# One register read per expert tile, moved into the step before it, in a graph-attention and mixture-of-experts kernel

## The chip, the cores and the metric

The kernel runs on one core of a Trainium2 chip. A core has five engines with an instruction queue each: TensorE (PE; its weight loads are listed as PEld), VectorE (DVE), ScalarE (ACT), GpSimd (POOL) and SyncE (SP). Each has a sequencer of its own that reads the instructions in their order; what the sequencer does itself, such as loading a register, is listed with a q (PEldq). The metric is the device time of one launch in microseconds, the median of several runs. A profiled execution gives the trace.

## The reference

A graph-attention layer with two heads over 6250 nodes and 100,000 edges, then a feed-forward layer in which each node goes to one of eight experts. Cut to what matters here:

```python
x = x + gat(layernorm(x), edges)               # segment sums over each node's edges
h = gelu(layernorm(x) @ W1 + b1)               # 6250 x 1024
probs = softmax(h @ Wg + bg)                   # over 8 experts
e = argmax(probs)
x = x + probs[e] * (h @ Wd[e] + bd[e])         # Wd: 8 x 1024 x 256, e differs from row to row
```

## The kernel before

The nodes are worked through in 49 blocks of 128. For each block GpSimd gathers the rows of its edges into `wg` in three parts of five, five and four tiles; VectorE and ScalarE weigh them (`weigh`); TensorE adds them up with a one-hot matrix (`add_up`, line 833) in PSUM. Small steps on the side find out which edges belong to the block: `prefix` (line 650, three matmuls of one column), `prefix_out` (653), `split` (662 on), `gather_late` (738), `choose` (745 to 756) and `spread` (761).

Four blocks make a phase. When a phase is summed, its rows go through the first feed-forward product (`g_hidden`, 916), the choice of expert (`g_logits` 954 to `g_place`) and are turned by TensorE (`g_rows`, 1039), copied by ScalarE (1040) and scattered to `by_expert`, a table in DRAM in which each expert has a list of its own. Full tiles of 128 rows of one expert are then taken out of it again, a phase later. `tabulate` makes, with VectorE, the table of the tiles that are ready: `where` (the tile's first row) and `who` (its expert). There are 55 such expert tiles: 1, then four a phase, and 14 in the last phase. For each, four steps run: `w_load` loads the rows (1126), `w_turn` turns them in two halves (1039, 1040), `w_expert` multiplies them by the expert's weights (1144 and 1146) and `w_out` makes the result `y` with VectorE (1160). In float32 a product shows as two passes in the profile, so the eight products of line 1146 are 16 matmuls.

Which expert it is, is known on the chip alone. So `w_expert` reads from `who` two numbers into registers of TensorE: the place of the expert's weights (line 1137) and of its bias (line 1140). The matmuls take their right-hand sides at these addresses, with a register instruction ahead of each (FUSED_REGOPS).

The order on every engine is written out by hand. `at(slot, place, fn, ...)` puts a step into a plan; the plan is sorted by slot and place, and the steps are called in that order, which is the order of every engine's queue. A block takes three slots, a phase twelve. `w_turn` has place 21, `w_expert` place 22 of the next slot, `add_up` place 32, `prefix` place 43. In the last phase no adding up is left, and turning and product alternate.

All of `w_turn`, `w_expert`, `g_rows`, `g_hidden` and `prefix` write to PSUM tiles named `pf`, of which there are three. A step that takes one over waits for its last reader.

## Time and profile before

| | us |
|---|---|
| median of 3 runs (lowest, highest) | 1330.88 (1330.65, 1338.22) |
| the profiled execution's own time | 1333.08 |
| its span, first to last instruction | 1331.3 |
| L1146 PE, products by expert weights, x880 | 204.6 busy |
| L833 PE, adding up, x1372 | 337.8 busy |
| L1144 PE, bias product, x55: TensorE idle before it | 8.0 in all: 5.5 "ACT wg L824", 1.4 "DVE idx L1158", 0.6 "DVE full_i L1068", 0.5 others |
| L761 PE: TensorE idle before it | 30.8, 17 times |
| mean granted TensorE clock | 0.934 |

A line of the timeline has the start, the duration, the engine, the line of the program, the operation, the tiles written and read, the number of instructions, and in brackets how long the engine stood idle before it and what ended that. Durations of the sequencer's own instructions are in the listings of single lines, as minimum, median and maximum in ns. The idle time named last in a list of waits is that of the semaphore that came last; it can be another's.

### The profile page before, as it was taken

How to read it: one execution, taken by the hardware profiler on the slowest of the kernel's cores; microseconds unless marked ns; L12 is line 12 of the kernel's file. 1: busy time of each engine (PE TensorE's matmuls, PEld its weight loads, DVE VectorE, ACT ScalarE, POOL GpSimd, SP SyncE). 2: the span in 40 equal slices, each digit the busy share in tenths (PEclk: the TensorE clock that was granted, in tenths of full speed). 3: DMA queues.
4: the chain of work that ended last, by engine and by line, in shares of the span. 5: the costliest groups of instructions: out<-in, count | busy, mean ns of one | idle time of the engine just before them, and what ended most of it. 6: DMA issues, size and time to landing. Idle time of an engine off the chain costs nothing. (4 is left out here: it accounts for less than half of the span.)

```text
span 1331.3 us, 22611 instructions
## 1 busy us (share of the span) xinstructions
PE 1133.9 (85%) x6551; PEld 873.9 (66%) x6551; DVE 971.6 (73%) x3521; ACT 679.9 (51%) x2011; POOL 840.3 (63%) x941
## 2 busy tenths in 40 slices
PE   4784677887978989989989899899898997998995
PEld 3563666665665775867757758677677586675784
DVE  6995889878797787877877977778779788651210
ACT  4782355546545546464565564555554646555221
POOL 1005777777777777777777776677766776626461
PEclk9796698898988999999999999899999998998998
DMA  4764866665555656665656566656566666646870
GB/s 147 227 193 122 234 186 187 205 191 171 174 171 183 216 178 200 195 205 174 207 170 204 177 205 189 192 175 189 183 190 198 181 196 195 191 128 231 293 236 16
DMA packets 115977, 249.77 MB, mean 188 GB/s; under 512 B 23372, under 2 KB 69656, under 8 KB 115702
## 3 DMA queue, kind: packets, MB, share of 16 engines
q0 software_dynamic: 44192, 131.04, 32.5%
q1 hardware_dynamic: 64342, 110.14, 26.5%
q10 hardware_dynamic: 7312, 7.05, 1.6%
q8 instruction: 56, 0.92, 0.3%
q14 instruction: 75, 0.61, 0.2%
HBM read 196.90 MB, written 57.97 MB: 191 GB/s over the span
## 5 line engine op out<-in xcount | busy, mean ns | idle before, releaser
L792 POOL DMA_INDIRECT wg<-table,dsti x686 | 675.1, 984 | 239.3 <-issue 169.7
L833 PE MATMUL p_a<-wg,hot 128*128 128x258 f32 x1372 | 337.8, 394 | 0.0
L833 PEld LDWEIGHTS p_a<-wg,hot 128*128 128x128 f32 x1372 | 263.7, 198 | 47.1 <-issue 9.2
L826 ACT ACTIVATE wg<-wg 128x128 f32<-128x128 f32 x686 | 216.6, 390 | 4.8
L916 PE MATMUL pf<-xT,w_sb 128*128 128x512 f32 (+1 forms) x416 | 199.4, 628 | 22.6 <-ACT xT L908 22.6
L1146 PE MATMUL pf<-wd_sb,half 128*128 x880 | 204.6, 386 | 0.0
L1146 PEld LDWEIGHTS pf<-wd_sb,half 128*128 128x128 f32 x880 | 162.7, 190 | 35.2 <-issue 10.1
L824 ACT COPY wg<-fix 128x10 f32<-128x10 f32 x147 | 25.0, 170 | 272.2 <-DVE wg L823 238.6
L916 PEld LDWEIGHTS pf<-xT,w_sb 128*128 128x128 f32 x416 | 81.2, 210 | 109.6 <-issue 80.1
L809 DVE TENSOR_TENSOR hot<-fix,loc 128x640 f32<-128x640 f32 x147 | 112.3, 764 | 25.1 <-ACT wg L824 24.6
L823 DVE TENSOR_TENSOR wg<-wg,fix 128x640 f32<-128x640 f32 x147 | 114.1, 776 | 5.1
L738 PE MATMUL pm<-rest,pick 128*128 128x33 f32 x588 | 82.2, 294 | 15.0 <-DVE place_i L666 15.0
L1040 ACT COPY half<-pf 128x512 f32<-128x512 f32 x110 | 60.8, 583 | 65.5 <-PE pf L1146 33.8
L918 ACT ACTIVATE hT<-pf,b_sb 128x512 f32<-128x512 f32 (+1 forms) x104 | 67.7, 659 | 47.1 <-PE pf L916 46.6
L1060 POOL DMA_INDIRECT by_expert<-row,place_i x47 | 49.4, 1052 | 65.3 <-ACT half L1040 18.3
L738 PEld LDWEIGHTS pm<-rest,pick 128*128 128x128 f32 x588 | 77.8, 211 | 15.7 <-issue 15.7
L456 PE MATMUL pf<-w_sb,xT 128*128 128x260 f32 x196 | 59.7, 432 | 18.6 <-ACT xT L450 18.6
L1040 ACT COPY row<-pf 128x512 f32<-128x512 f32 x94 | 52.3, 586 | 40.6 <-PE pf L1039 39.6
L1039 PE MATMUL pf<-ident,hT 128*128 128x128 f32 x392 | 59.0, 289 | 14.5 <-ACT row L1040 13.2
L704 ACT ACTIVATE wt<-tm,hot_e 128x128 f32<-128x128 f32 x196 | 66.4, 386 | 9.2 <-DMA tm<-terms 9.2
L619 POOL DMA_INDIRECT win<-keys,first x49 | 50.1, 1022 | 32.7 <-DMA keys<-keyb 14.2
L662 DVE TENSOR_SCALAR pick<-iota_s,late 128x768 f32<-128x768 f32 x49 | 30.8, 628 | 48.8 <-ACT late L653 48.8
(274 smaller groups left out, 1794.0 us busy)
## 6 DMA issues: line engine op xcount, KB each, us to landing
row<-by_expert SPq DMA_DIRECT2D x39, 641.0 KB
lbc<-lrow SPq DMA_DIRECT2D x49, 448.0 KB
wg<-table,dsti POOLq DMA_INDIRECT x686
wg<-by_expert SPq DMA_DIRECT2D x16, 641.0 KB
wd_sb<-in_L_ffn_Wd_dram SPq DMA_DIRECT2D x8, 1024.0 KB
tm<-terms SPq DMA_DIRECT2D x49, 128.0 KB
table<-tb ACTq DMA_DIRECT2D x12, 520.0 KB
xs<-in_x_dram SPq DMA_DIRECT2D x12, 512.0 KB
```

Source lines behind the costliest of these rows:

```text
L456: nc.tensor.matmul(pW[:, :TW], xT[:, k * P:(k + 1) * P], w_sb[:, k, :], start=(k == 0), stop=(k == KC - 1))
L704: nc.scalar.activation(kept[b]["wt"][:, g, h, :], tm[:, h, :], AF.Identity, scale=hot_e[:, g, 1, h:h + 1])
L738: nc.tensor.matmul(pk[:, c, :], k["pick"][:, c * P:(c + 1) * P], k["rest"], start=True, stop=True)
L792: nc.gpsimd.indirect_dma_start(out=wg[:, t - QS[q], :], out_offset=None, in_=table[:, :], in_offset=bass.IndirectOffsetOnAxis(ap=kept[b][" ...
L809: nc.vector.tensor_tensor(hot[:, :n], iota_ps.unsqueeze(1).to_broadcast([P, n, P]), kept[b]["loc"][:, QS[q]:QS[q + 1]].unsqueeze(2).to_bro ...
L823: nc.vector.tensor_mul(wg[:, :, :D], wg[:, :, :D], p_w[:, :, 0:1].to_broadcast([P, n, D]))
L826: nc.scalar.activation(wg[:, t, D2:SE], wg[:, t, D2:SE], AF.Identity, scale=wg[:, t, D + 1:D2])
L833: nc.tensor.matmul(sums[b], hot[:, t - QS[q], :], wg[:, t - QS[q], :SE], start=(t == 0), stop=(t == T - 1))
L916: nc.tensor.matmul(ph[:, :w], wt["w1"][:, k, j * P:(j + 1) * P], xT[:, k, :w], start=(k == 0), stop=(k == KC - 1))
L918: nc.scalar.activation(hT[:, j, :w], ph[:, :w], AF.Gelu, bias=wt["b1"][:, j:j + 1])
L1040: nc.scalar.copy(o, pT)
L1146: nc.tensor.matmul(py[:, :C], res[k]["half", i, j // 4][:, j % 4, :], wt["wd"][:, ds(wo[0] + j * C, C)], start=False, stop=(j == KH - 1))
```

## The change

`who` keeps one number per tile, the expert's number times C (256). It serves as the bias' place, and eight times it, worked out in the register instructions, as the weights' place. So TensorE reads one register per expert tile, in `w_ask`. This read is called at one of three places:

- A step at place 31.9 of the slot in which the tile is turned, one slot before its product, puts the tile on the list `asked`. The next `add_up` reads the register after its third product and empties the list.
- If no `add_up` came in between, `w_expert` reads it itself, ahead of its products.
- In the last phase the tiles but the first stand in the set `follows`: their register is read inside the product of the tile before, ahead of its sixth product of eight.

```diff
@@ add_up
             for t in range(QS[q], QS[q + 1]):
                 nc.tensor.matmul(sums[b], hot[:, t - QS[q], :], wg[:, t - QS[q], :SE],
                                  start=(t == 0), stop=(t == T - 1))
+                if t == QS[q] + 2:
+                    for k, i in asked:
+                        w_ask(k, i)
+                    asked.clear()
@@ tabulate
-            who = res[k]["who"] = fw.tile([1, NMAX, 2], I32, name="who")
-            nc.vector.tensor_scalar(who[:, :n, 0], tab_f[:1, 0, :], float(KH * C), None, op0=ALU.mult)
-            nc.vector.tensor_scalar(who[:, :n, 1], tab_f[:1, 0, :], float(C), None, op0=ALU.mult)
+            who = res[k]["who"] = fw.tile([1, NMAX], I32, name="who")
+            nc.vector.tensor_scalar(who[:, :n], tab_f[:1, 0, :], float(C), None, op0=ALU.mult)
@@ before w_expert
+        def w_ask(k, i):
+            _, at_row = nc.values_load_multi_w_load_instructions(
+                res[k]["who"][0:1, i:i + 1], engines=[PE], min_val=0, max_val=(NX - 1) * C,
+                skip_runtime_bounds_check_because="an expert's number, at most NX - 1, times C")
+            res[k]["of", i] = at_row[0]
+
+        asked, follows = [], set()
@@ w_expert
-            who = res[k]["who"]
-            reason = "an expert's number, at most NX - 1"
-            _, wo = nc.values_load_multi_w_load_instructions(
-                who[0:1, i, 0:1], engines=[PE], min_val=0, max_val=(NX - 1) * KH * C,
...
-            _, bo = nc.values_load_multi_w_load_instructions(
-                who[0:1, i, 1:2], engines=[PE], min_val=0, max_val=(NX - 1) * C,
...
+            if asked:
+                w_ask(*asked.pop())
+            of = res[k].pop(("of", i))
             py = res[k]["py", i] = pff.tile([P, 512], F32, name="pf")
-            nc.tensor.matmul(py[:, :C], ones_bf[:3, :], bd3[:, ds(bo[0], C)], start=True, stop=False)
+            nc.tensor.matmul(py[:, :C], ones_bf[:3, :], bd3[:, ds(of, C)], start=True, stop=False)
             for j in range(KH):
+                if j == KH - 3 and (k, i + 1) in follows:
+                    w_ask(k, i + 1)
                 nc.tensor.matmul(py[:, :C], res[k]["half", i, j // 4][:, j % 4, :],
-                                 wt["wd"][:, ds(wo[0] + j * C, C)], start=False, stop=(j == KH - 1))
+                                 wt["wd"][:, ds(of * KH + j * C, C)], start=False, stop=(j == KH - 1))
@@ the plan
                 at(t, 21, w_turn, k, i)
+                if last and i:
+                    follows.add((k, i))
+                else:
+                    at(t, 31.9, asked.append, (k, i))
                 at(t + 1, 22, w_expert, k, i)
```

More of the change, by code (lines that the diff above doesn't have):

```diff
@@ L1132, in w_turn @@
                 turn_half(half.rearrange("p j t -> p (j t)"), lambda j: sr[:, j * P:(j + 1) * P], h)
-        def w_expert(k, i):
-            who = res[k]["who"]
-            reason = "an expert's number, at most NX - 1"
-            _, wo = nc.values_load_multi_w_load_instructions(
-                who[0:1, i, 0:1], engines=[PE], min_val=0, max_val=(NX - 1) * KH * C,
-                skip_runtime_bounds_check_because=reason)
-            _, bo = nc.values_load_multi_w_load_instructions(
-                who[0:1, i, 1:2], engines=[PE], min_val=0, max_val=(NX - 1) * C,
-                skip_runtime_bounds_check_because=reason)
+        def w_ask(k, i):
[4 more added lines that the diff above has]
+        asked, follows = [], set()
+        def w_expert(k, i):
+            if asked:
+                w_ask(*asked.pop())
+            of = res[k].pop(("of", i))
             py = res[k]["py", i] = pff.tile([P, 512], F32, name="pf")
-            nc.tensor.matmul(py[:, :C], ones_bf[:3, :], bd3[:, ds(bo[0], C)], start=True, stop=False)
+            nc.tensor.matmul(py[:, :C], ones_bf[:3, :], bd3[:, ds(of, C)], start=True, stop=False)
             for j in range(KH):
+                if j == KH - 3 and (k, i + 1) in follows:
+                    w_ask(k, i + 1)
                 nc.tensor.matmul(py[:, :C], res[k]["half", i, j // 4][:, j % 4, :],
-                                 wt["wd"][:, ds(wo[0] + j * C, C)], start=False, stop=(j == KH - 1))
+                                 wt["wd"][:, ds(of * KH + j * C, C)], start=False, stop=(j == KH - 1))
             for h in range(2):
```

## The prediction

> **What bounds the kernel now.** I read the page's busy shares first, then the waits of TensorE, then its timeline around each product, and last what the other engines do while it stands.

> ```profile
> PE 1133.9 (85%) x6551; PEld 873.9 (66%) x6551; DVE 971.6 (73%) x3521; ACT 679.9 (51%) x2011; POOL 840.3 (63%) x941
> ```

> No engine is full. The kernel runs in phases of four blocks; from 440 to 1155 us one takes about 88.7 us, of which TensorE computes some 81. So TensorE is nearly, not wholly, the bound, and what a removed gap is worth depends on what it meets next.

> The reads that the change is about, from the listings of their two lines (PEldq is TensorE's sequencer; duration min/median/max in ns):

> ```profile
> L1137 PEldq TENSOR_LOAD <-who x55: 297/305/693, 356.2 to 1308.5; - x55
> L1140 PEldq TENSOR_LOAD <-who x55: 295/295/497, 356.8 to 1308.9; - x55
> ```

> One pair goes ahead of each of the 55 products. With windows on single products these listings show, for the one at 620.76 us: first read at 618.9, second at 619.3, address arithmetic at 619.7, first matmul at 620.8. Each read costs the sequencer 0.40 us from start to start, two 0.80, but TensorE was still working off queued matmuls: no gap. Its timeline shows where that cover fails:

> ```profile
> 645.32 0.28 PE L1144 MATMUL pf<-bd,ones_bf 3*128 x1
> ...
> 657.99 1.14 PE L1039 MATMUL pf<-ident,hT 128*128 128x128 f32 x8 [0.20 <-ACT half L1040]
> 659.32 0.16 PE L650 MATMUL pf<-over,before_bf 128*128 128x1 bf16 x1 [0.19 <-ACT row L1040]
> ...
> 660.22 0.26 PE L1144 MATMUL pf<-bd,ones_bf 3*128 x1 [0.69 <-ACT wg L824]
> ```

> The third product of this phase (645.32) starts without a gap, the fourth (660.22) after 0.69 us: the sequencer stood at the tiny matmuls of L650 until 659.32, then had two reads to do and nothing queued. The list of TensorE's waits has 5.5 us in 8 such gaps, one a phase. ACT, which it names, is only the last semaphore seen; the reads started at 659.3 and 659.7.

> [...] So a register read holds up issue, not the array, while the queue lasts; the trace agrees (0.80 us of reads, no gap at 620.76; 0.69 us at 660.22). [...] the lead seen here, from the first read to the product's matmul, is 1.6 to 2.8 us in the covered cases of a phase. [...] The `pf` tiles are such banks, three in rotation, so whoever gets one waits for its last reader; the 1.39 us gap below is that.

> **What the gap at 660.22 meets next.** One timeline over all engines, 658 to 682 us:

> ```profile
> 658.68 1.07 ACT L1040 COPY row<-pf 128x512 f32<-128x512 f32 x2
> ...
> 661.64 0.14 ACT L653 COPY late<-pf 128x3 f32<-128x3 f32 x1
> ...
> 661.81 0.62 DVE L662 TENSOR_SCALAR pick<-iota_s,late 128x768 f32<-128x768 f32 x1 [0.34 <-ACT late L653]
> ...
> 673.20 0.16 DVE L755 TENSOR_SCALAR late_i<-got 128x6 int32<-128x6 int32 x1
> ...
> 673.39 0.20 ACT L756 CAST loc<-late_i 128x6 f32<-128x6 int32 x1 [0.38 <-DVE late_i L755]
> ...
> 673.64 0.28 PE L761 MATMUL pm<-ident,loc 128*14 128x128 f32 x1 [2.07 <-ACT loc L756]
> ```

> VectorE starts at 661.81 on what L650 gave, and works without a break of note (10.54 busy of 11.60 us in that stretch) until 673.4; only then can TensorE go on at L761, after standing for 2.07 us. Between the two, TensorE has no other gap and nothing on VectorE waits for its product. Time won at 660.22 is therefore lost at 673.64.

> **The change, part by part.**
> 1. *The fourth product of each phase, 8 times.* Its read moves ahead of L650, into the adding up. In the built program its first matmul also waits for the second of the two row copies (ACT, 658.68 + 1.07 = 659.75), so it can start at about 659.80 instead of 660.22: 0.42 us. All of it goes into the wait at L761, which should grow from 2.07 to about 2.5. On the path: 0. If it carried: 8 x 0.42 = 3.4 us.
> 2. *The other 29 reads inside an adding up, and 13 inside a product.* They were covered and stay so. The read follows three products of two passes of 0.218 us, that is 1.3 us of queued work, against 0.40. Tightest is the fourth product's adding up: TensorE stood until 654.96, then eight transposes and six passes follow to 657.2. The sequencer's visible pace in a product (8 address steps from 660.2 to 661.3, about 0.15 us each) puts the read at 656.6 and its end at 657.0. Cost 0, with 0.2 us to spare. If the cover fails, 0.40 each. Behind the read stand the remaining matmuls of the adding up; only `finish` waits for them. Inside the last products the cover is larger: five products of 0.43 us against 5 x 0.15.
> 3. *Wait of a read for VectorE.* Only the first of each phase waits for `who`. It was written at 607.0 and will be read about 618: cover 11 us.
> 4. *Address arithmetic.* The built program has as many fused register instructions, 495, each with one operation more in 440 of them (42 ns with two operations, 46 to 51 with three): some 5 ns, hidden, since the pace stays far below the 0.43 us of a product.
> 5. *VectorE loses 12 conversions.* 0.08 us each from start to start. In a phase it lies at 695.8, and VectorE idles at 707.1 for a DMA (1.50 us): 0. Upper bound 12 x 0.08 = 1.0 us.
> 6. *The tail.* Here TensorE is the path to the end: the chain of waits from 1235 us on is products and transposes with little else. Three gaps, from TensorE's, ScalarE's and VectorE's timelines:

> ```profile
> 1229.44 0.26 PE L1144 MATMUL pf<-bd,ones_bf 3*128 x1 [0.64 <-DVE full_i L1068]
> ...
> 1235.62 0.27 PE L1144 MATMUL pf<-bd,ones_bf 3*128 x1 [1.39 <-DVE idx L1158]
> ...
> 1250.20 0.27 PE L1144 MATMUL pf<-bd,ones_bf 3*128 x1 [0.25 <-issue]
> ```
> ```profile
> 1233.88 0.58 ACT L1040 COPY half<-pf 128x512 f32<-128x512 f32 x1 [1.58 <-PE pf L1039]
> ```
> ```profile
> 1235.09 0.47 DVE L1160 SCALAR_TENSOR_TENSOR y<-pf,row 128x256 f32<-128x256 f32 x1
> ```

> At 1229.44 one read of two remains (no adding up follows any more): -0.40. At 1235.62 the built program shows a side effect: the banks of PSUM are dealt out otherwise. Before, the product takes the bank that VectorE frees with `y` (1235.09 + 0.47 = 1235.56), which stood behind the making of the table. After, it takes the one that ScalarE frees with `half` (1233.88 + 0.58 = 1234.46), and the next transposes, near 1238, take the other, free by then. That is 1235.62 - 1234.52 = -1.10. At 1250.20 one read is left: arithmetic at 1249.7 instead of 1250.1, and the matmul follows the transposes (1247.97 + 1.99 = 1249.96) with the 0.07 us of overlap that gapless products show (1240.34 after transposes until 1239.37 + 1.04), at 1249.89: -0.31. The later products have no gap from reads. Loads of the last phase's rows are issued from 1239.3 and used from 1248 on, so 1.8 us less does not meet them.

> **Sum:** 0 in the phases, -0.40 - 1.10 - 0.31 = -1.81 us in the tail. The profiled execution has a span of 1331.3 us and a time of 1333.08; they become 1329.5 and 1331.3. The median of three runs, 1330.88, is 2.2 below that execution; minus 1.8 it is **1329.1**.

> **Rivals.**
> *A. The gaps carry (0.20).* If the stretch from L650 to L761 has play, the 8 x 0.42 = 3.4 us come on top: 1325.7, with the conversions 1324.7 at the lowest. For it: TensorE's 85%, and that it works through from 680 to 729 us. Against: the 2.07 us at L761, alike in the phase at 1120.
> *B. The bank swap gives nothing (0.10)*, because the wait for `y` only moves to the next transposes, or a load comes late: -0.40 - 0.31 = -0.7, 1330.2.
> *C. Slower: the reads in the adding up are not covered (0.12).* Mechanism: the sequencer arrives at the read with under 0.40 us of matmuls queued, as after the stalls of TensorE at 640.4 and 654.96 us, so that the third and fourth product of each of some nine phases pay 18 x 0.40 = 7.2: 1330.88 + 7.2 - 1.8 = 1336.3. It decides when the sequencer needs over 0.17 us an instruction there. All 37 exposed would be +14.8 - 1.8 = +13.0, 1343.9. Against: 0.15 us in the product.
> *D. It doesn't do what it says:* excluded by the built program, 111 reads become 56, the last a flag. Left over for the clock, granted at 0.94 to 0.98 in most phases and free to move: 0.03.

> **Numbers.** The forecast has 0.55 (1327.5 to 1330.5 by itself). The range, 1325.0 to 1333.5, takes in A and B, most of the spread and a fraction of C's stalls. A measurement of this kernel can tell about 1%, 13 us: all gaps ahead of products together are 8 us, so faster by more has 0.02; slower by more needs nearly all of C, 0.02; within it 0.96.

> **What would show it.** Right: the fourth product of a phase after a gap near 0.3 instead of 0.69, L761 after 2.5 instead of 2.07, phases still 88.7 us; the 1.39 gap shrunk to about 0.3. A: L761's gap unchanged and phases of 88.2. C: new gaps ahead of L833 or behind it. Wrong in any case: a phase longer or shorter by over 0.5 us at the same granted clock.

## The result, and the profile after

The changed kernel is **slower by a little, not faster**: 1341.20 us against 1330.72 us (medians of 22 runs each), ratio 1.0072 with a 95% interval of 1.0054 to 1.009. The range ended at 1333.5. Two repeats in other sets of runs gave 1.0020 (1.0001 to 1.0039) and 1.0016 (0.9988 to 1.0044; this interval takes in 1). So the change costs some 0.2 to 0.7%, 2 to 10 us. Single runs of one kernel scatter by 13 to 19 us, so one profiled execution alone says little; each count below is taken over several.

The profiled execution of the result has a span of 1333.1 us (time 1334.93) and is one of the quickest of its 22. A repeat of the same kernel, e1_again, was profiled in the slowest of its 22 (span 1344.1, time 1345.97, median 1339.66). The two lie near the two ends of the scatter. First lines of the pages, after and repeat:

```profile
PE 1135.9 (85%) x6551; PEld 874.1 (66%) x6551; DVE 970.3 (73%) x3509; ACT 680.7 (51%) x2011; POOL 842.1 (63%) x941
```
```profile
PE 1147.6 (85%) x6551; PEld 883.3 (66%) x6551; DVE 970.8 (72%) x3509; ACT 681.0 (51%) x2011; POOL 841.0 (63%) x941
```

The same 6551 matmuls kept TensorE busy for 1133.9 us before, 1135.9 in the quick execution and 1147.6 in the slow one. The rest of the span, TensorE's idle time, is 197.4, 197.2 and 196.5 us. So in all TensorE doesn't wait longer: the matmuls themselves last longer. The other engines differ by 2 us at most.

What the change says it does is in the profile after, where lines 1039, 1144 and 1146 have become 1043, 1150 and 1154. TensorE's timeline around the fourth product of a phase and the wait behind it (columns as in the section on the profile before), the listing of the read's line, and two rows of the groups (at their end: busy us, mean ns, idle time before them):

```profile
665.62 0.16 PE L650 MATMUL pf<-over,before_bf 128*128 128x1 bf16 x1 [0.19 <-ACT row L1044]
...
666.11 0.26 PE L1150 MATMUL pf<-bd,ones_bf 3*128 x1 [0.27 <-ACT row L1044]
...
679.76 0.38 PE L761 MATMUL pm<-ident,loc 128*14 128x128 f32 x1 [2.29 <-ACT loc L756]
```
```profile
L1138 PEldq TENSOR_LOAD <-who x55: 296/302/913, 355.8 to 1310.0; - x55
```
```profile
L833 PE MATMUL p_a<-wg,hot 128*128 128x258 f32 x1372 | 339.4, 395 | 0.0
L1154 PE MATMUL pf<-wd_sb,half 128*128 x880 | 204.6, 386 | 0.0
```

One read per tile; the gap at the fourth product is 0.27 us instead of 0.69; and neither the adding up nor the products ever stand idle, so the moved reads are covered everywhere. The tail's three gaps shrank as well (0.64, 1.39 and 0.25 before; 0.23, 0.29 and none after):

```profile
1232.50 0.26 PE L1150 MATMUL pf<-bd,ones_bf 3*128 x1 [0.23 <-DVE place L1033]
1237.58 0.26 PE L1150 MATMUL pf<-bd,ones_bf 3*128 x1 [0.29 <-ACT half L1044]
...
1252.15 0.28 PE L1150 MATMUL pf<-bd,ones_bf 3*128 x1
```

From the first product of the tail (1229.44 before, 1232.50 after) to the last expert tile the kernel before takes 82.0 to 82.3 us (three profiles), the changed one 80.6 to 80.9. The eight phases, from the fourth product of one to that of the last, take 703.5, 703.7 and 706.0 us before, but 707.6, 713.5 and 716.4 after. In these profiles that is where most of the time is lost.

**What is lost there.** A table by stretches shows it (columns: start and end; length; busy us of PE, PEld, DVE, ACT and POOL with instructions; granted TensorE clock; DMA share; GB/s). The clock in the records changes on a grid of 3413 ns (all but the last of the 58 records of the profile before, and of the 62 of the one after, last a whole number of such steps, 54 of them a single one), so the stretches are laid on that grid. The kernel before, from the adding up ahead of L761 to the first hidden layer:

```profile
754.99:758.40 3.41, 3.41 (x46) 3.35 (x42) 3.00 (x15) 1.45 (x5) 2.51 (x3) 1.00 0.41 111
758.40:761.82 3.42, 1.87 (x9) 1.30 (x7) 3.04 (x18) 2.66 (x6) 2.80 (x3) 1.00 0.41 114
761.82:765.23 3.41, 2.68 (x21) 2.20 (x21) 3.34 (x14) 1.96 (x6) 2.50 (x4) 1.00 0.43 95
765.23:768.64 3.41, 0.95 (x5) 0.71 (x6) 1.39 (x9) 2.63 (x7) 2.43 (x4) 1.00 0.85 277
768.64:772.06 3.42, 3.42 (x5) 1.35 (x5) 3.10 (x7) 3.34 (x9) 2.57 (x3) 0.50 1.09 399
772.06:775.47 3.41, 3.41 (x16) 2.15 (x14) 0.64 (x2) 2.19 (x7) 2.54 (x3) 1.00 0.63 182
```

and the same phase of e1_again:

```profile
766.60:770.02 3.42, 3.42 (x33) 3.31 (x33) 2.97 (x16) 1.45 (x5) 2.50 (x4) 1.00 0.42 109
770.02:773.43 3.41, 1.40 (x7) 0.88 (x5) 3.07 (x18) 2.66 (x6) 2.79 (x3) 1.00 0.41 113
773.43:776.84 3.41, 3.13 (x15) 2.92 (x16) 3.34 (x12) 1.93 (x5) 2.51 (x3) 0.50 0.39 99
776.84:780.26 3.42, 1.54 (x12) 1.06 (x10) 1.08 (x8) 1.75 (x4) 1.41 (x3) 1.00 0.75 183
780.26:783.67 3.41, 2.66 (x3) 1.18 (x4) 2.32 (x5) 3.36 (x11) 2.80 (x3) 0.50 1.02 398
783.67:787.08 3.41, 3.41 (x5) 1.35 (x4) 1.66 (x4) 1.53 (x2) 2.50 (x4) 0.50 0.70 209
787.08:790.50 3.42, 3.42 (x16) 2.35 (x15) 0.14 (x1) 2.69 (x10) 2.52 (x3) 1.00 0.43 115
```

Read the first busy number and the clock together. Where TensorE computed 0.95 of 3.41 us (0.28), the next stretch has half the clock, and the products of the hidden layer run at half speed in it: their matmuls start 0.85 us apart in it (769.10, 769.96, 770.81) and 0.43 us apart behind it (772.29, 772.72, 773.15). Where it computed 1.87 us (0.55, the stretch with the wait at L761 before), the clock stays. In e1_again the wait at L761 left 1.40 us (0.41): the clock halves there too, and this phase has three stretches at half clock instead of one. A stretch at half clock is called a halving below.

Over fourteen profiles (three of before, three of after, eight of the experiments below; 440 to 1180 us) the count is clear: of full-clock stretches with a busy share under 0.40, 98 of 98 are followed by one at half clock; from 0.40 to 0.43, 13 of 16; from 0.43 to 0.60, 14 of 67; above, 4 of 2703. So more than 2.05 us of idle time (0.60 of 3.41) in one stretch was followed by a halving each time, and less of it sometimes. What sets off the other halvings, the four above 0.60 above all, was not found.

In each profile, all half-clock stretches after 440 us start on one such grid, to 2 ns. No gap of TensorE from 440 to 1190 us is over 2.75 us; one gap of 2.3 us (2.29 in e1_again, ahead of the half clock at 773.43), or two shorter ones (0.68 and 1.96 us before, ahead of the one at 768.64), were enough.

**Why the change meets it.** From L650 to L761 a phase takes about 13.93, 14.09 or 14.29 us (once 14.55), before and after alike. TensorE has worked off what lies between the two after 12.20 us before and 11.80 after, and waits for the rest: 1.72, 1.87 to 1.93 or 2.03 to 2.09 us in 24 phases of before, 2.13, 2.29 or 2.50 (once 2.75) in 24 phases after. So the removed 0.42 us went into the wait, as predicted. The mean wait grew by less, from 1.97 to 2.30 us, since the middle size is the most frequent after and the largest before. And it went across 2.05: before, 13 of 24 waits are over it, by 0.04 at most; after, all are. An estimate: were the grid's position at each wait left to chance, 2.05 us of one wait g would fall into one stretch in (3.41 + g - 4.10) / 3.41 of the cases: 0.41 at 2.08, 0.47 at 2.29, nothing under 2.05. That makes some 5 halvings in 24 phases before and 11 after. Counted behind L761: 2, 1 and 1 of 8 before (4 of 24); 4, 7 and 5 of 8 after (16 of 24). The median phase with a halving behind L761 takes 90.0 us (17 phases), the median one without it 88.6 (25); six of the 25 take over 89.2 for other halvings or causes that were not followed. (The last of the eight phases, which is shorter, is left out of this.)

**Does it hold beyond the profiles?** Two of the three profiles of the changed kernel, e1_again and a_fourth, are the slowest executions of their sets, so they overstate the difference. But the mean granted clock of every timed execution is on record. In the set of e1_again it is 0.9340 before (56 executions) and 0.9282 after (22), in that of a_fourth 0.9335 (51) and 0.9303 (14); one halving takes 0.0013 off it (half of 3.41 us in 1331), so some 2.5 to 4.5 more halvings are usual, by this estimate. A straight line through both kernels' executions of a set gives 0.8 us for 0.001 of clock. At equal clock the changed kernel differs by -0.3 us (give or take 1.2) and +0.5 us (give or take 1.7), where the mean times differ by 4.3 and 2.9 us. So the loss goes with the clock. For e3 and e2, described below, the same line leaves 1.8 us each (give or take 1.3 and 1.5), for which the runs show no cause.

### The profile page after: what moved, and what is told of

Its sections match the earlier page's. It is cut to its first block, busy times and chain, and to the rows that moved or that the text cites. A ratio compares the mean times of both kernels' runs of the same rounds, so it can differ in the third digit from the quotient of the medians.

```text
span 1333.1 us, 22544 instructions
## 1 busy us (share of the span) xinstructions
PE 1135.9 (85%) x6551; PEld 874.1 (66%) x6551; DVE 970.3 (73%) x3509; ACT 680.7 (51%) x2011; POOL 842.1 (63%) x941
## 5 line engine op out<-in xcount | busy, mean ns | idle before, releaser
L833 PE MATMUL p_a<-wg,hot 128*128 128x258 f32 x1372 | 339.4, 395 | 0.0
L833 PEld LDWEIGHTS p_a<-wg,hot 128*128 128x128 f32 x1372 | 264.4, 199 | 47.7 <-issue 8.6
L920 PE MATMUL pf<-xT,w_sb 128*128 128x512 f32 (+1 forms) x416 | 199.2, 628 | 22.7 <-ACT xT L912 22.7
L1154 PE MATMUL pf<-wd_sb,half 128*128 x880 | 204.6, 386 | 0.0
L1154 PEld LDWEIGHTS pf<-wd_sb,half 128*128 128x128 f32 x880 | 162.6, 190 | 30.1 <-issue 4.9
L824 ACT COPY wg<-fix 128x10 f32<-128x10 f32 x147 | 25.0, 170 | 276.7 <-DVE wg L823 193.0
L920 PEld LDWEIGHTS pf<-xT,w_sb 128*128 128x128 f32 x416 | 81.1, 210 | 109.0 <-issue 79.5
L738 PE MATMUL pm<-rest,pick 128*128 128x33 f32 x588 | 79.3, 288 | 15.5 <-DVE place_i L666 15.4
L738 PEld LDWEIGHTS pm<-rest,pick 128*128 128x128 f32 x588 | 74.8, 204 | 16.2 <-issue 16.2
L662 DVE TENSOR_SCALAR pick<-iota_s,late 128x768 f32<-128x768 f32 x49 | 30.8, 630 | 52.0 <-ACT late L653 51.9
```

What stands on the lines that cost most here:

```text
L738: nc.tensor.matmul(pk[:, c, :], k["pick"][:, c * P:(c + 1) * P], k["rest"], start=True, stop=True)
L833: nc.tensor.matmul(sums[b], hot[:, t - QS[q], :], wg[:, t - QS[q], :SE], start=(t == 0), stop=(t == T - 1))
L920: nc.tensor.matmul(ph[:, :w], wt["w1"][:, k, j * P:(j + 1) * P], xT[:, k, :w], start=(k == 0), stop=(k == KC - 1))
L1154: nc.tensor.matmul(py[:, :C], res[k]["half", i, j // 4][:, j % 4, :], wt["wd"][:, ds(of * KH + j * C, C)], start=False, stop=(j == KH - 1))
```

## The experiments

Sets of runs share the kernel before on their own chip, so ratios are compared, not microseconds across sets. "Half" is the number of halvings from 440 to 1190 us in the profile, then those behind L761 (of 8 phases). They are of one execution each: those of e5 and e12 are among the three quickest of 22, that of e4 is the quickest of its 5, those of e7 and e8 are the slowest of their 6.

| run | median us | ratio to before (95%) | half; behind L761 |
|---|---|---|---|
| before: profile, b_again, b_third | 1330.7, 1335.1, 1338.0 | 1; 0.9990 (0.9963-1.0016); 1.0006 (0.9987-1.0025) | 11, 9, 9; 2, 1, 1 |
| after: profile, e1_again, a_fourth | 1341.2, 1339.7, 1339.3 | 1.0072, 1.0020, 1.0016 (above) | 13, 18, 17; 4, 7, 5 |
| e2_gap_back | 1341.7 | 1.0048 (1.0027-1.0069) | 17; 6 |
| e3_one_read | 1340.9 | 1.0041 (1.0021-1.0061) | 15; 5 |
| e5_two_reads | 1337.8 | 1.0014 (0.9991-1.0036) | 14; 4 |
| e4_rows_first | 1320.4 | 0.9881 (0.9859-0.9904) | 5; 0 |
| e7_xT_first | 1288.8 | 0.9620 (0.9586-0.9654) | 6; 4 |
| e8_old_xT_first | 1286.8 | 0.9611 (0.9577-0.9645) | 2; 0 |
| e12_useless | 1330.6 | 0.9966 (0.9950-0.9981) | 7; 0 |
| e13_useless2 | 1318.8 | 0.9879 (0.9836-0.9922) | 0; 0 |

**Repeats.** The changed kernel again:

> The changed kernel once more, for a profile of a typical execution (median 1341.2 us against 1330.7 before). Theory 1, the clock: the wait of TensorE ahead of L761 grew from 2.07 to 2.3-2.5 us, and the clock record shows a second stretch of 3.4 us at half clock in more of the phases, each about 1.5 us; expected 1336 to 1344, with phases of 88.3-88.8 us where one such stretch lies, 89.5-91 where two or more lie, and no new gap at L833 or L1154. Theory 2, the moved reads hold TensorE up: gaps of 0.2-0.4 us ahead of L833 or L1154 in some 18 to 37 places, phases of 89.5 or more whatever the clock. Theory 3, the first 440 us (no read lies there but one): the phases are 88.7 and the loss lies before 440 us.

and the kernel before:

> The kernel before once more, for its profile. Theory 1 (the clock): the same rule as in the profiles so far: a stretch of 3413 ns on a fixed grid in which TensorE computes under about 0.43 of the time is followed by one at half clock; 1 to 4 of the 8 waits at L761 are; phases of 88.6-88.8 us with one half-clock stretch, 89.5-91 with more. Rival: half-clock stretches as many as in the changed kernel (5 to 7 of 8), and the difference lies elsewhere. Time 0.998 to 1.002.

> The kernel before a third time, for its profile: half-clock stretches behind L761 in 0 to 4 of 8 phases (3 of 16 so far) if theory 1 holds; 5 to 7 if the difference between the kernels lies elsewhere. Time 0.998 to 1.002.

> The changed kernel once more, beside e12 and e13. Theory 1: 1.002 to 1.007 of the time before, a second half-clock stretch in 5 to 7 of 8 phases. Rival (chance): 0.999 to 1.001, with stretches as few as before.

All fit theory 1, except that both repeats of the changed kernel lie nearer to 1 than the first result, and a_fourth's interval takes in 1. The time until the first of these fourth products, with only five reads in it, scatters between 481 and 491 us over all kernels (before 482.9 to 488.5, after 487.6 to 490.8), also from half-clock stretches: theory 3 is not excluded for a part, and the runs don't settle how much of those 3 to 4 us is chance.

**Is it the moved reads?** One read, left where it was:

```diff
         def w_expert(k, i):
-            if asked:
-                w_ask(*asked.pop())
+            w_ask(k, i)
```

> One read in place of two, but ahead of its own product as before: none is moved. Theory 1 (clock): the gap at the fourth product shrinks to about 0.3 us and the wait at L761 grows to 2.3-2.5 us as in the changed kernel, so it is slower than before all the same, 1337 to 1343 us. Theory 2 (moved reads): 1329 to 1331 us. Theory 3 (address arithmetic, conversions): as the changed kernel, 1341 us; it is told from theory 1 by e2.

1.0041, gap 0.28 us, waits at L761 of 2.12 to 2.70. The loss is there without a moved read, so moving isn't the cause. The reverse, getting the old gap back by two reads at the fourth product, was tried twice. The first edit (reading twice in `w_expert` where `asked` still holds something) doesn't reach that product, whose read is done in the adding up:

> The changed kernel, with the read ahead of the fourth product of a phase (and of the first one of the tail) made twice, so that the old gap comes back there; the 42 moved reads stay moved. Theory 1 (clock): gap 0.69 again, L761 after 2.07 us again, as few half-clock stretches as before, and 1329 to 1332 us. Theory 2 (the moved reads hold TensorE up) and theory 3 (something else in the new program, such as the address arithmetic): nothing comes back, 1341 to 1344 us.

The gap stayed at 0.28, so e2 says nothing on theory 1; it is a further changed kernel (1.0048). Its profile has 55 reads, one a tile as after: of the doubled call no second read is left. The second edit keeps the fourth tile off the list:

```diff
+            if ("of", i) not in res[k]:
+                w_ask(k, i)
+                w_ask(k, i)
...
-                else:
+                elif last or i < n - 1:
                     at(t, 31.9, asked.append, (k, i))
```

> The changed kernel, with the fourth product's read taken out of the adding up and made twice ahead of that product, so that its old gap of 0.69 us comes back; the other 41 reads stay moved. (The edit of e2 did not reach this product: its read was already done in the adding up.) Theory 1 (the clock): L761 after 2.07 us, clean phases of 88.7 us again, the second half-clock stretch in 1 to 4 of 8 phases, 0.996 to 1.001 of the time before. Rival (the moved reads or the new program cost it): 1.002 to 1.007 as the changed kernel, whatever that gap is.

This profile too has 55 reads, so the fourth product has one read ahead of it here and not two. But this read starts only behind the first matmul of L650 (663.79 us, L650 at 663.63), after a semaphore wait of the sequencer, where e3's starts with it (both at 668.57). So the gap came back by a part only, to 0.43 to 0.53 us, and the waits at L761 lie between (1.88 to 2.15, one 2.59). So do the halvings, 4 of 8, and the ratio, 1.0014 (0.9991 to 1.0036). The direction fits, but the interval holds both sides: the reverse is not shown by time.

**Filling the wait.** The eight transposes of `g_rows` for a phase's third block stand behind L761, with data that is long ready. They go ahead of it:

```diff
-                        ((v + 10, 38), (v + 11, 38), (v + 13, 38), (v + 13, 39))[i])
+                        ((v + 10, 38), (v + 11, 38), (v + 13, 33.3), (v + 13, 39))[i])
```

> The changed kernel, with the eight transposes of g_rows for the third block of a phase put ahead of L761 instead of behind it; their data is long there, so they fill TensorE's wait. Theory 1 (clock): the wait at L761 falls under 0.7 us, the half-clock stretch that begins 13-15 us after the fourth product goes in all phases, and the kernel comes back at least to the time before, 1331 us or less; if the waits behind L761 (0.68 and 1.96 us) don't grow by what is filled, up to 8 x 1.6 = 13 us less than that, 1318. Theory 2 (moved reads): only the filled idle time counts, so not below 1341 - 13 = 1328, and new gaps at the reads remain.

1320.4: the wait at L761 is 1.25 to 1.61 us, more than the 0.7 expected, but no halving lies behind it. The waits behind stayed (0.68 and 1.95), so four phases still have the halving behind L920: three of them take 88.0 to 88.1 us (the fourth is the shorter last one), those without one 86.0 to 86.3. In e7 the copies of the fourth block go behind the copies that L920 waits for as well (its place 39 becomes 46):

> e4, and also the row copies of the fourth block (g_rows, place 39) put behind the two copies that the first hidden layer waits for (L912, place 45), so that ScalarE makes those first. Theory 1: no wait of TensorE of over 1.7 us is left in a phase and none of the 8 phases has a half-clock stretch: 84 to 86 us a phase, 1296 to 1308 us. If only idle time counted (no clock), e4's 1320 falls by at most the wait of 1.95 us at L920, 8 times: not under 1305, with phases of 86 and 88 as in e4.

1288.8, below what was expected. Its timeline:

```profile
576.90 1.04 PE L1043 MATMUL pf<-ident,hT 128*128 128x128 f32 x8
579.40 0.28 PE L761 MATMUL pm<-ident,loc 128*14 128x128 f32 x1 [1.47 <-ACT loc L756]
579.89 1.14 PE L907 MATMUL pf<-ident,xnf 128*128 128x128 f32 x8 [0.21 <-ACT row L1044]
581.01 1.09 PE L1043 MATMUL pf<-ident,hT 128*128 128x128 f32 x8
581.94 3.60 PE L920 MATMUL pf<-xT,w_sb 128*128 128x512 f32 x8
```

The wait of 1.95 us ahead of L920 is gone and the one of 0.68 behind L761 too; a new one of up to 0.91 us stands ahead of L650. One point missed: four of its phases still have a halving behind L761, behind stretches with shares of 0.41 to 0.57. The kernel before with the same two moves:

> The kernel before with the same two moves of g_rows as e7: against e7 it shows what the change is worth when the clock is not halved. Theory 1: the change is then a gain, the 1.8 us of the tail and 8 x 0.2 to 0.4 us in the phases: e7 is faster than this kernel by 2 to 5 us. Rival (the moved reads cost something by themselves): e7 is slower than this kernel, by 3 to 10 us.

The two can't be told apart (0.9620 and 0.9611, intervals of 0.7 points): **the gain expected of the change was not there**. The profiles show two effects that cancel. TensorE idles for 171.1 us of e7's span and 175.0 of e8's; the tail's gain is in this (82.4 us from its first product to the last in e8, 80.6 in e7). But it is busy for 1118.7 us in e7 and 1115.2 in e8: e8 waits 0.84 to 1.21 us at L761 and has no halving in a phase; e7 waits some 0.4 us longer, 1.25 to 1.81, and has those four, and its eight phases take 673.7 us against 668.3.

**Is it the clock, or the idle time?** e4 and e7 shorten idle time as well as keeping the clock. To part the two, work was added: eight transposes into the tile that `g_rows` overwrites next, ahead of L761 (e9 and e12; e10 is the kernel before with the same); in e11 and e13 eight more, ahead of the first hidden layer. Each set of eight goes into eleven phases. Nothing else moves.

```diff
+        def g_ahead(k, i):
+            pT = res[k]["ahead", 0] = pff.tile([P, 512], F32, name="pf")
+            for j in range(8):
+                nc.tensor.transpose(pT[:, j % 4 * P:(j % 4 + 1) * P], hT[:, j % 4, i * P:(i + 1) * P], ident)
...
+                if i == 2 and not last:
+                    at(t, 33.3, g_ahead, k, i)
```

> The changed kernel with work added: eight transposes ahead of L761 in each phase, whose result is written over before anyone reads it. Nothing else moves. Theory 1 (the clock): the wait at L761 falls from 2.1-2.5 to 1.1-1.5 us, a half-clock stretch behind it in 0 to 1 of 8 phases instead of 5 to 7, phases of 88.3-88.8 us; 1329 to 1334 us, some 6 us less than the changed kernel in the same call, though TensorE does more. Rival (time is lost only by work and waits): nothing is gained, the same as the changed kernel or later.

> The kernel before with the same eight transposes. Theory 1: the wait at L761 of 1.7-2.1 us falls to 0.7-1.1, the few stretches behind it (3 in 16 phases) go; 1330 to 1333 us; e9 is then faster than this kernel by the 1.8 us of the tail, within the scatter. Rival: the same as the kernel before or later.

> e9 with eight more useless transposes, ahead of the first hidden layer's matmuls in phases 1 to 8 (the wait of 1.96 us for the xT copies). Theory 1: no half-clock stretch is left in most phases: 86.6-87.0 us a phase (one such phase of the kernel before, without a half-clock stretch, took 86.8), so 8 x 1.7 = 13 us less than e9: 1315 to 1322 us. Rival: later than the changed kernel, by up to 8 x 1 us.

> The changed kernel a third time, on the chip of e9 to e11. Theory 1: 1.002 to 1.007 of the time before, with a second half-clock stretch in 5 to 7 of 8 phases. Rival (the difference was chance): 0.999 to 1.001, with stretches as few as before.

This set ran where every kernel was slower by a quarter: before 1652.6, e9 1656.2 (0.9978), e10 1663.3 (1.0028), e11 1670.5 (1.0105), the changed kernel 1652.3 (1.0032, 1.0005 to 1.006). Here the forecasts of theory 1 failed: e9 gains nothing that is clear of the scatter, and e11, with the most work added, is the slowest. Phases took 111 to 121 us there. TensorE stood idle between the matmuls of one adding up (L833, 12.6 to 22.4 us in all, 0.0 in before and after) and ahead of weight loads for nothing that the profile shows (53.8 us ahead of those of L717 in the profile of a_third, 5.3 in the one of the result), and in several phases L761 had no wait at all. Why it was so wasn't found; e1_again's set, on the same chip, had not been slow. Where there is no wait at L761 nothing can be filled, so the set is left out of the counts. The same two kernels on another chip, beside a_fourth (1339.3):

> e9 again (the changed kernel with eight useless transposes ahead of L761 in each phase), on a chip whose kernel before takes 1330 to 1336 us. Theory 1 (the clock): the wait at L761 1.1-1.5 us, a half-clock stretch behind it in 0 to 1 of 8 phases, phases of 88.3-88.8 us, and some 6 us less than the changed kernel in the same call though TensorE does more. Rival (only work and waits count): the same as the changed kernel or later.

> e11 again (eight more useless transposes, ahead of the first hidden layer in phases 1 to 8). Theory 1: no half-clock stretch is left in most phases, 86.6-87.0 us each, 13 us less than e12. Rival: later than the changed kernel, by up to 8 us.

e12: 1330.6, 8.7 us below the changed kernel. e13: 1318.8, 20.5 below. Each has more work for TensorE in eleven phases, the same order, and is faster; their intervals lie below that of a_fourth. TensorE's timeline in e12, with the added transposes (L1062) and the wait behind them:

```profile
675.14 1.04 PE L1062 MATMUL pf<-ident,hT 128*128 128x128 f32 x8
677.60 0.28 PE L761 MATMUL pm<-ident,loc 128*14 128x128 f32 x1 [1.42 <-ACT loc L756]
```

The mean granted clock of the timed executions is 0.937 in e12 against 0.930 in a_fourth. Stretches of e13 around L761 and L920:

```profile
758.03:761.44 3.41, 1.68 (x14) 1.45 (x15) 3.31 (x14) 2.48 (x7) 2.76 (x3) 1.00 0.41 111
761.44:764.86 3.42, 2.07 (x18) 1.59 (x16) 2.42 (x11) 1.85 (x5) 2.10 (x4) 1.00 0.63 140
764.86:768.27 3.41, 3.22 (x13) 1.69 (x11) 2.21 (x5) 3.36 (x11) 2.68 (x3) 1.00 0.99 320
768.27:771.68 3.41, 3.41 (x16) 2.25 (x15) 1.76 (x4) 3.37 (x9) 2.50 (x4) 1.00 1.04 315
```

None of them falls under 0.49, and from 440 to 1190 us there is not one half-clock stretch; phases take 87.1 to 87.6 us, a little above the 86.6 to 87.0 expected. With this it is shown, and not only argued, that waits of this size cost TensorE its clock and that filling them gives it back. That the change's 0.42 us makes such waits more frequent rests on the counts (4 against 16 of 24) and on the recorded clocks; the kernel before with the added work was run only in the set that was slower by a quarter.

## Why the prediction was wrong

1. *The fourth product.* The move of the gap was right: 0.69 became 0.27, and the 0.42 us went into the wait at L761, though that is 2.29 us in most phases and not the 2.5 forecast. The step that failed is its last sentence but one, **"On the path: 0"**. A wait was taken as time that passes and nothing more. It was the longest wait of the phase, 2.07 us, and what came on top put TensorE's busy share under 0.40 in one stretch of the clock's grid in 15 of 24 phases: 13, 18 and 17 halvings in the profiles instead of 11, 9 and 9. At full loss one takes half of 3.41 us, 1.7, as the clock in it is 0.50. The phases of the profiles lost 8.1 us on average (712.5 against 704.4) with 16.0 - 9.7 = 6.3 more halvings, 1.3 us each. Over all timed executions of the two later sets the loss is smaller, 4.3 and 2.9 us, as two of the profiles are of the slowest executions.
2. *The other reads.* Right: no idle time ahead of L833 or L1154, and e3 loses as much with no read moved. Rival C, with 0.12, had the sign right and the cause wrong: no read was left uncovered.
3. *The wait for `who`, address arithmetic, conversions.* Right as far as the profile shows: no gap in the products, VectorE 970.3 us busy instead of 971.6, and nothing on the path follows from it.
4. *The tail.* Predicted -1.81; of it -0.40 at the start and -1.41 behind it. Found: the first gap 0.41 smaller, the rest 1.1 to 1.7 us shorter. But e2, with the same order of products, waits 1.63 us at the second one as the kernel before does. e3, with no read moved, waits 0.29 us there as the changed kernel does. So the swap of the banks isn't tied to the moved reads; how a build deals them out was not followed.
5. *Rival A* (the gaps carry) is out, as the wait at L761 grew by what the gap lost. *The clock* was named as "granted at 0.94 to 0.98 in most phases and free to move" and given 0.03 as a leftover. It needed a mechanism: the granted clock of the profile before fell to 0.50 right behind this very wait in two of eight phases. The "about 88.7 us" of a phase hid it: from the fourth product of one phase to that of the next, two of the first seven took 90.7 and 90.0 us, and both hold two halvings. The others took 88.4 to 88.8.

That the time would stay within 1% had 0.96 and holds in each set of runs. It rests on how small all gaps ahead of products are; that the clock's cost also stayed under 1% was not reasoned, and so partly luck.

## What to carry to other kernels

Before a wait is called free because something else sets the end, lay TensorE's busy time over the granted clock in short stretches: here waits brought stretches of 3.41 us under a busy share of 0.40, and each of these was followed by one at half clock (98 of 98), in which a matmul of the hidden layer started every 0.85 us instead of 0.43. Taking one small gap away can merge idle time into one long wait; here waits of 0.7 and 2.1 us were cheaper than waits of 0.3 and 2.3. Where a long wait can't be shortened, put ready work into it; moving two steps of `g_rows` made this kernel 3.8% faster with the change and 3.9% without it.
